# A four-stage block kernel: norm moves one cycle sooner, operands on another queue, stores kept back, weight lows on one engine

## The chip, the cores and the metric

The kernel runs on one core of a Trainium2 chip as one program. The metric is the device time of one execution in microseconds (us). Before the change three runs took 958.97 to 959.96 us, with a median of 959.61 us.

A core has five engines with an instruction queue each: TensorE (PE; its weight loads are listed as PEld), VectorE (DVE), ScalarE (ACT), GpSimd (POOL) and SyncE (SP). Each works through its own queue in order and waits at semaphores for the others. Transfers are issued here from SP's queue and from GpSimd's queue, and run on 16 DMA engines.

## The reference, cut to what matters

`x` is 2 x 1024 tokens of 512 numbers, float32.

```python
x = x + attn_a(layernorm(x))   # 4 heads, gated linear attention in chunks of 128 tokens
x = x + ffn(layernorm(x))      # 512 -> 1408 -> 512, integer weights with scales
x = x + attn_b(layernorm(x))   # one head of 512, softmax over 1024 keys, no mask
x = x + ffn(layernorm(x))      # the same ffn weights again

def attn_b(x):                 # per batch
    Q, K, V = x @ W_q, x @ W_k, x @ W_v
    return softmax(Q @ K.T / sqrt(512)) @ V @ W_o

def ffn(x):
    W = lambda wq, s: (wq - 128.0) * s[:, None]
    h = silu(x @ W(wq_gate, s_gate).T) * (x @ W(wq_up, s_up).T)
    return h @ W(wq_down, s_down).T
```

## The kernel before, in words

**Numbers in two parts.** A float32 operand `v` is split into `hi` (ScalarE's cast to the rounded type `fp32r`, line 70) and `lo = v - hi` (a subtraction, line 71, on VectorE unless the call names GpSimd). `mm3` multiplies with three matmuls: hi by hi, hi by lo, lo by hi (lines 84 to 86). `load_split` loads a tile and splits it.

**Order.** The kernel is written as one list of steps. A planner then gives each engine its queue: it takes the steps in the order of writing, simulates their times with a cost model, and lets a later step go ahead on an engine where an earlier one isn't ready in the simulation. The queues that come out are fixed; on the chip each engine keeps to its own. `behind(inss)` holds instructions of its block behind given ones of the same engine. `array(fn)` does this for TensorE, so that the matrix work of the second attention goes in the order written. Tiles come from pools; a tile with a tag waits for the release of an earlier one with the tag, and a pool that is opened after others are closed takes their memory, so that its first writes wait for the last readers there. `wp` has 12 slots of 8 KB a partition for large operands. `psum` has eight banks.

**Stage 1, attn_a.** First `M = W_q W_k^T` for the second attention is computed (`weight_product`, into four PSUM banks `pM`), and `spill` splits it (casts on ScalarE, lows on VectorE) and stores it to `m_d` with eight DMAs. Meanwhile the first norm tiles are made and turned (`ln_tile`, tiles `xn_a`, `pxT_a`, `xh_a`, `xl_a`), and `load_wqkv` splits Wk, Wq and Wv, the odd ones of four on GpSimd. `kv_part` and `q_head` are the projections (`pWk`, `pWv`, `pq`), `gate_proj` and `gates` the gates (`pab`, `ab`, `pz`). Sixteen chunks follow. The last steps compute `W_v W_o` (`V`), which `spill` stores to `vo_d`, and prepare the first FFN's operands.

**Stages 2 and 4, the FFN** (names end in `f` and `g`). Two rounds `pr` of 1024 tokens. Each runs over 11 blocks `j` of hidden units, with seven products instead of eight of half-size blocks (`products`, tiles `pX`, `pY`, `pZ`, `pV`, line 326); then eight tiles of the down product (`po`, lines 881 and 882). `stationary(j, ...)` provides the weights of block j in a slot `wc`: in the first round of stage 2 it loads integer codes (`cg`, `cu`), casts them, and GpSimd forms four sums and differences (lines 309 to 312), and SP stores the result to `wc_d[j]` (line 313, 896 KB); later it loads them back (line 315). `finish` makes the hidden tiles `ha`, `hb` (pool `ffnh`) and their splits `hs` (pool `ffn1`). `combine` makes the token operands from the transposed tokens `xT`.

**Norm groups.** For the second attention and the FFNs a norm is taken in groups of four tiles: `ln_steps` gives eight steps, four `ln_norm` (load `xin`, statistics `bn`, the power `rs` on GpSimd, `xn`, and a transpose by 32 x 32 blocks into `y`) and four `ln_move`, each of four DMAs of 64 KB that put the blocks in place in `xT`. `y` has one buffer, `xin` two.

**Stage 3, attn_b** (per batch b). `v_tile` and `q_proj`, then four cycles of two query tiles each: `scores_head` (products `ps`, whose sums end at `summed`), the matrix work `between`, `scores_tail` with the softmax (`mx`, `nm`, `pe`). `probs_T` turns a tile of probabilities: a transpose by blocks on VectorE (`py`), a store to `p_d` (`p<-py`, 512 KB) and four reads (`raw<-p`), all on SP. `probs_split` makes `pth` and `ptl` of it, and `out_b(b, i)` is the product with V (`pob`). The residual rows `xrb` come on GpSimd's queue. `do(norm, n)` takes the next n norm steps, `do(moving, n)` the next n of `combine`.

In batch 1 the norm group of stage 4 is taken along: group 0 before cycle 0, two norms of group 1 after cycle 0, and the other two with all four moves after cycle 1. In batch 0 the second group's four norms are all taken before cycle 1, and its moves after it.

Of the kernel before, what the change touches and what calls it, by code (L numbers as in the profile page):

```python
# [9 lines left out]
F32 = mybir.dt.float32  # L10
F32R = mybir.dt.float32r
I32 = mybir.dt.int32
AF = mybir.ActivationFunctionType
# [21 lines left out]
def hybrid_block_kernel(ctx: ExitStack, tc: tile.TileContext, a, out):  # L35
# [25 lines left out]
    def behind(inss):  # L61

        es = ExitStack()
        for ins in inss:
            es.enter_context(tc.issue_after(ins))
        return es
# [20 lines left out]
        ends[id(ps)] = end  # L87
        return end

    ends, normed_x, parts = {}, [], []  # L90

    def new_xT(name):
        return tuple(slot(f"{n}_{name}").rearrange("p (k c) -> p k c", k=KD) for n in ("xh", "xl"))
# [96 lines left out]
    def ln_move(nm, st, b):  # L190

        if b == 0:
            lnT[nm, st] = slot(f"xT_{nm}{st}").rearrange("p (k c) -> p k c", k=KD)
        y = lnY[nm, st]
        xf = lnT[nm, st].bitcast(F32).rearrange("p k (i b q) -> p (k i) b q", i=ST, b=4)
        for c in range(4):
            sync = nm in "af" or (nm, st) in (("b", 0), ("b", 1), ("g", 3)) or ((nm, st) == ("b", 2) and c % 2)
            (nc.sync if sync else nc.gpsimd).dma_start(  # L198
                out=xf[32 * b : 32 * (b + 1), :, c, :],
                in_=y[32 * c : 32 * (c + 1), b].rearrange("p k i q -> p (k i) q"),  # L200
            )
# [94 lines left out]
        codes(sp, "stg", c, a["wd"][j], f"cd{j}")  # L296
        nc.sync.dma_start(out=wd_d[j], in_=c)

    def stationary(j, name, fresh=None, loaded=None):


        w = slot(f"wc{name}_{j}").rearrange("p (n c) -> p n c", n=8)
        if fresh or loaded:
            a21, a11, s1, s2, s3, a12, s4, a22 = (w[:, n] for n in range(8))
            for n, (dst, nm) in enumerate(((w[:, 1:6:4], "cg"), (w[:, 0:8:7], "cu"))):
                room = (loaded[n], None) if loaded else fresh
                codes(*room, dst, a["wgu"][j][:, n * 512 : (n + 1) * 512], f"{nm}{name}_{j}")
            f = lambda x: x.bitcast(F32)
            nc.gpsimd.tensor_tensor(s1, f(a21), f(a22), ALU.add)
            nc.gpsimd.tensor_tensor(s2, f(s1), f(a11), ALU.subtract)  # L310
            nc.gpsimd.tensor_tensor(s3, f(a11), f(a21), ALU.subtract)
            nc.gpsimd.tensor_tensor(s4, f(a12), f(s2), ALU.subtract)
            nc.sync.dma_start(out=wc_d[j], in_=f(w[:, 1:8]))
        else:
            nc.sync.dma_start(out=w[:, 1:8].bitcast(F32), in_=wc_d[j])
        return w

    def products(ps, w, nm, pr, n, first):
# [17 lines left out]
    with ExitStack() as actx:  # L336
# [42 lines left out]
        def load_wqkv(nm, staged=None):  # L379
            two = [slot(f"{nm}{n}") for n in range(2)]  # L380
            done = []
            wqkv[nm] = [two[k // 2][:, k % 2 * 1024 : (k % 2 + 1) * 1024] for k in range(KD)]
            for k in range(KD):
                w, eng = wqkv[nm][k], nc.gpsimd if k % 2 else None
                if staged is None:
                    _, load = load_split(w, sp, a[nm][k * P : (k + 1) * P, :], f"{nm}{k}", eng)
                else:
                    done.extend(split(w[:, 0:512], w[:, 512:1024], staged[:, k], eng))
            return load if staged is None else done
# [90 lines left out]
        def q_head(st, h):  # L480
# [8 lines left out]
            for k in range(KD):  # L489
# [7 lines left out]
                    k == 0,  # L497
                    k == KD - 1,
                )
            nc.scalar.activation(qTa[st][:, h, :], ps, AF.Identity, bias=bq_s[:, h : h + 1])  # L500
            if h == 1:
                gates(st)
            if h == 2 and st > 0:
# [183 lines left out]
            wq_loaded = nc.sync.dma_start(out=staged[:, m], in_=a["Wq"][m * P : (m + 1) * P, :]).ins  # L687
        with behind((end,)):
            kv_part(0, "Wk")
        with behind(load_wqkv("Wq", staged)):  # L690
            spill(ap, ("kT", "kw", "sdec", "at"), pm, m_d, "M")
        for i in range(4):
            ends.clear()
            q_head(0, i)
            with behind((wq_loaded, *ends.values())):
                for t in ((), (4,), (5,), (6, 7))[i]:
                    ln_tile(t)
        load_wqkv("Wv")
        kv_part(0, "Wv")
        decays(0)  # L700
# [69 lines left out]
    def ffn(src, dst, nm, wcs, moving, ended, after):  # L770

        with ExitStack() as fctx:
            fh = fctx.enter_context(tc.tile_pool(name=f"ffnh{nm}", bufs=1))
            f1 = fctx.enter_context(tc.tile_pool(name=f"ffn1{nm}", bufs=2))
            fw = fctx.enter_context(tc.tile_pool(name=f"ffnw{nm}", bufs=KH))
            fp = fctx.enter_context(tc.tile_pool(name=f"ffn{nm}", bufs=4))
            wd = []
            for pr in range(2):  # L780
# [47 lines left out]
                for j in range(KH):  # L828
# [21 lines left out]
                    with behind(ended if pr == 0 and j < 3 else ()):  # L850
                        while moving:
                            moving.pop(0)()
                        first = nm == "f" and pr == 0
                        plan = (0, 1, 1, 1, 2, 2, 2, 1, 1, 1, 2) if first else (1, 1, 1, 1, 2, 2, 1, 1, 1, 1, 2)
                        for _ in range(plan[j] if early else 0):
                            early.pop(0)()

                    late_wd = nm == "f" and j < KH - 1
                    for n in range(len(wd), max(0, 2 * (j - 4)) if late_wd else KH if nm == "f" else j + 1):
# [50 lines left out]
    with ExitStack() as bctx:  # L910
# [230 lines left out]
        for b in range(NB):  # L1141
# [35 lines left out]
            for i in (0, 1):  # L1177
                probs_T(b, i)
            do(norm, 2)
            cycle(b, 1, lambda: q_proj(b, 1, (2, 3)))  # L1180
            for i in (2, 3):
                probs_T(b, i)
            do(norm, 4 if b == 0 else 6)
            array(out_b, b, 0)
            if b:
                moving = combine("g", 0)
# [25 lines left out]
            do(moving, 6)  # L1212
        array(out_b, 1, 5)
        array(out_b, 1, 6)
        wcs = [stationary(n, "g0") for n in range(2)]
        ended = (array(out_b, 1, 7),)

    out_t = [out[t * P : (t + 1) * P, :] for t in range(NT)]
# [63 lines left out]
```

## Time and profile before

| | |
|---|---|
| median of 3 runs | 959.61 us (958.97 to 959.96) |
| the profiled execution | 959.36 us, its span 957.6 us, granted clock 0.995 |
| PE busy | 937.2 us, 98% |
| DVE, ACT, POOL busy | 724.8 us (76%), 411.4 us (43%), 235.4 us (25%) |
| DMA | 162.18 MB, 169 GB/s over the span |

The profile comes from one execution. Times inside it count from the start of the span. An entry such as `pob<-vh,pth` names the output tile and what it reads; `[4.28 <-ACT pth L70]` says that the engine was idle 4.28 us before it and that ScalarE's line 70, which wrote `pth`, ended that. SPq and POOLq are the queues from which SP and GpSimd issue transfers. The granted clock is TensorE's, as a share of full speed. A matmul's record covers its pipeline, so one of 0.39 us may start 0.23 us after the last; what counts for TensorE is the distance from start to start.

### The profile page before, as it was taken

To read this page: it belongs to the slowest core of one execution; us is meant where nothing else is said; L and a number is where in the kernel's file an instruction comes from. 1 tells how busy PE (TensorE), PEld (TensorE's weight loads), DVE (VectorE), ACT (ScalarE), POOL (GpSimd) and SP (SyncE) were. 2 spreads that over 40 slices of the span, in tenths; PEclk is the share of its full clock that TensorE was granted. 3 is DMA by queue.
4 is the path that set the end of the run, shared out by engine and by line. 5 is a ranking of instruction groups with operands and counts; after the bars stand their busy time and mean duration, and the time that the engine had idled before them with its cause. 6 is when DMAs were issued, how large, how long until landed. Compare 5 with 4: busy or idle time off the path is not lost.

```text
span 957.6 us, 13198 instructions
## 1 busy us (share of the span) xinstructions
PE 937.2 (98%) x4402; PEld 776.1 (81%) x4402; DVE 724.8 (76%) x1457; ACT 411.4 (43%) x795; POOL 235.4 (25%) x334
## 2 busy tenths in 40 slices
PE   9999999999999999999999999999988999999998
PEld 7788888888788878888888788888866888888887
DVE  7757767779999699778948778479764967976655
ACT  6544434335665344354234444244332443534421
POOL 6323323444563012110120402041400261001100
PEclk9999999999999999999999999999989999999999
DMA  9426456576798557733745979247966772573112
GB/s 338 158 90 160 148 122 174 190 188 203 283 356 274 119 178 270 202 51 142 263 79 85 172 162 242 66 79 154 184 123 228 288 194 53 186 256 132 39 61 84
DMA packets 214838, 162.18 MB, mean 169 GB/s; under 512 B 150961, under 2 KB 166641, under 8 KB 214769
## 3 DMA queue, kind: packets, MB, share of 16 engines
q1 hardware_dynamic: 211184, 152.41, 54.8%
q0 software_dynamic: 3584, 8.92, 4.8%
q8 instruction: 35, 0.57, 0.3%
q14 instruction: 35, 0.28, 0.1%
HBM read 104.76 MB, written 41.84 MB: 153 GB/s over the span
## 4 chain that ended last, share of the span: by engine, by line
PE 84%; DVE 6%; DMA 5%; SPq 3%; ACT 1%; issue 1%; POOL 0%; ACTq 0%; DVEq 0%
PE pog L882 4%; PE pog L881 4%; PE pVg L326 4%; PE pZg L326 4%; PE pXg L326 4%; PE pVf L326 4%; PE pof L882 4%; PE pof L881 4%; PE pXf L326 4%; PE pZf L326 4%; PE pob L86 2%; PE pob L84 2%; PE pob L85 2%; PE pYg L326 2%; PE pYf L326 2%; PE psV L980 2%
## 5 line engine op out<-in xcount | busy, mean ns | idle before, releaser
L881 PE MATMUL pog<-wdg,hsg 128*128 128x512 f32 (+1 forms) x165 | 60.3, 375 | 0.0
L882 PE MATMUL pog<-wdg,hsg 128*128 128x512 f32 (+1 forms) x165 | 60.2, 375 | 0.0
L881 PE MATMUL pof<-wdf,hsf 128*128 128x512 f32 x154 | 59.5, 390 | 0.7 <-ACT hsf L70 0.7
L882 PE MATMUL pof<-wdf,hsf 128*128 128x512 f32 x154 | 59.2, 390 | 0.0
L84 PE MATMUL pob<-vh,pth 128*128 128x512 f32 x128 | 51.3, 401 | 5.2 <-ACT pth L70 5.2
L86 PE MATMUL pob<-vh,ptl 128*128 128x512 f32 x128 | 51.0, 398 | 0.0
L85 PE MATMUL pob<-vl,pth 128*128 128x512 f32 x128 | 50.9, 397 | 0.0
L326 PE MATMUL pXg<-B_g,wcg 128*128 128x512 f32 x176 | 47.1, 392 | 3.4 <-DMA wcg<-wc 3.4
L71 POOL TENSOR_TENSOR hsg<-sgg,hsg 128x128 fp32r<-128x128 f32 x40 | 19.6, 509 | 124.7 <-ACT hsg L70 124.7
L326 PE MATMUL pVf<-T_f,wcf 128*128 128x512 f32 x176 | 46.4, 390 | 1.0 <-ACT hbf L811 1.0
L326 PE MATMUL pVg<-T_g,wcg 128*128 128x512 f32 x176 | 46.4, 389 | 0.0
L326 PE MATMUL pXf<-B_f,wcf 128*128 128x512 f32 x176 | 45.9, 391 | 0.4 <-DMA wcf<-wc 0.4
L109 POOL TENSOR_TENSOR rs_b<-ve_b,mhalf 128x1 f32<-128x1 f32 x16 | 12.3, 775 | 121.0 <-DVE ve_b L107 121.0
L326 PEld LDWEIGHTS pXg<-B_g,wcg 128*128 128x128 f32 x176 | 33.0, 188 | 10.7 <-DMA wcg<-wc 3.8
L326 PEld LDWEIGHTS pVf<-T_f,wcf 128*128 128x128 f32 x176 | 32.9, 188 | 8.3 <-ACT hbf L811 1.4
L198 POOL DMA_DIRECT2D xT_g<-y_g x48 | 31.1, 655 | 34.0 <-DVE T_b L71 21.0
L326 PEld LDWEIGHTS pXf<-B_f,wcf 128*128 128x128 f32 x176 | 32.9, 188 | 7.6 <-DMA wcf<-wc 0.8
L326 PEld LDWEIGHTS pVg<-T_g,wcg 128*128 128x128 f32 x176 | 33.0, 188 | 6.9
L70 ACT CAST pth<-raw 128x512 fp32r<-128x512 f32 x30 | 17.1, 618 | 49.5 <-DMA raw<-p 49.4
L1086 POOL DMA_DIRECT2D xrb<-x x16 | 9.2, 573 | 109.4 <-DMA x<-xrb 62.4
L881 PEld LDWEIGHTS pog<-wdg,hsg 128*128 128x128 f32 x165 | 31.1, 188 | 5.7
L882 PEld LDWEIGHTS pog<-wdg,hsg 128*128 128x128 f32 x165 | 31.0, 188 | 5.6
(337 smaller groups left out, 2767.5 us busy)
## 6 DMA issues: line engine op xcount, KB each, us to landing
wcg<-wc SPq DMA_DIRECT2D x22, 896.0 KB, 6.1
wc<-wcf SPq DMA_DIRECT2D x11, 896.0 KB, 5.7
wcf<-wc SPq DMA_DIRECT2D x11, 896.0 KB, 6.0
p<-py SPq DMA_DIRECT2D x15, 512.0 KB, 3.8
raw<-p SPq DMA_DIRECT2D x60, 128.0 KB, 4.1
xin_a<-in_x SPq DMA_DIRECT2D x16, 256.0 KB, 4.7
xra<-in_x SPq DMA_DIRECT2D x16, 256.0 KB, 2.7
row<-cl SPq DMA_DIRECT2D x16, 256.0 KB, 3.9
```

Of the source, the lines that this page charges most:

```text
L70: c = nc.scalar.copy(hi, src)
L71: return c.ins, (eng or nc.vector).tensor_tensor(lo, src, hi.bitcast(F32), ALU.subtract).ins
L84: nc.tensor.matmul(ps, lhs_hi, rhs_hi, start=first, stop=False)
L85: nc.tensor.matmul(ps, lhs_hi, rhs_lo, start=False, stop=False)
L86: end = nc.tensor.matmul(ps, lhs_lo, rhs_hi, start=False, stop=last).ins
L109: nc.gpsimd.tensor_tensor(rs, ve, mhalf, ALU.pow)
L198: (nc.sync if sync else nc.gpsimd).dma_start(out=xf[32 * b : 32 * (b + 1), :, c, :], in_=y[32 * c : 32 * (c + 1), b].rearrange("p k i q -> ...
L326: nc.tensor.matmul(ps, w[:, m, k * P : (k + 1) * P], o[:, s, k, :], start=first and k == 0 and s == 0, stop=k == 1 and s == 1, skip_group_ ...
L881: nc.tensor.matmul(ps, hs[i][0][:, j], wd[j][:, ds], start=j == 0, stop=False)
L882: nc.tensor.matmul(ps, hs[i][1][:, j], wd[j][:, ds], start=False, stop=j == KH - 1)
L980: ends[nm] = nc.tensor.matmul(ps, o[:, i, k], w[:, j, k], start=first and k == 0 and i + j == 0, stop=k == 1 and i == 1, skip_group_check= ...
L1086: nc.gpsimd.dma_start(out=xr, in_=x2[t])
```

## The change

- `load_wqkv`: the odd lows of Wk and Wq go from GpSimd to VectorE; those of Wv stay.
- `spill` of M is taken after the second head of `q_head(0, ..)`, behind its copy on ScalarE and the last norm on VectorE, and no longer right after the Wq splits.
- `stationary`: the store of line 313 is put on a list, and the FFN's block loop takes the oldest off it as long as more than two are left, and all in the last block.
- The pools `ffn1` and `ffnh` are opened in the other order, in both FFNs.
- `ln_move`: of the first norm group of stage 4 (`("g", 0)`) half of the DMAs go to SP, as already for `("b", 2)`.
- In batch 1 the third and fourth norm of group 1 are taken in cycle 1 after `q_proj`, behind the sums of the scores; after cycle 1 only the four moves are left.
- The first two operands `wc` of stage 4 are loaded from GpSimd's queue.

```diff
--- before.py
+++ after.py
@@ -87,7 +87,7 @@
         ends[id(ps)] = end
         return end
 
-    ends, normed_x, parts = {}, [], []
+    ends, normed_x, parts, copied = {}, [], [], []
 
     def new_xT(name):
         return tuple(slot(f"{n}_{name}").rearrange("p (k c) -> p k c", k=KD) for n in ("xh", "xl"))
@@ -194,7 +194,8 @@
         y = lnY[nm, st]
         xf = lnT[nm, st].bitcast(F32).rearrange("p k (i b q) -> p (k i) b q", i=ST, b=4)
         for c in range(4):
-            sync = nm in "af" or (nm, st) in (("b", 0), ("b", 1), ("g", 3)) or ((nm, st) == ("b", 2) and c % 2)
+            half = (nm, st) in (("b", 2), ("g", 0))
+            sync = nm in "af" or (nm, st) in (("b", 0), ("b", 1), ("g", 3)) or (half and c % 2)
             (nc.sync if sync else nc.gpsimd).dma_start(
                 out=xf[32 * b : 32 * (b + 1), :, c, :],
                 in_=y[32 * c : 32 * (c + 1), b].rearrange("p k i q -> p (k i) q"),
@@ -296,7 +297,9 @@
         codes(sp, "stg", c, a["wd"][j], f"cd{j}")
         nc.sync.dma_start(out=wd_d[j], in_=c)
 
-    def stationary(j, name, fresh=None, loaded=None):
+    saves = []
+
+    def stationary(j, name, fresh=None, loaded=None, queue=None):
 
 
         w = slot(f"wc{name}_{j}").rearrange("p (n c) -> p n c", n=8)
@@ -310,9 +313,9 @@
             nc.gpsimd.tensor_tensor(s2, f(s1), f(a11), ALU.subtract)
             nc.gpsimd.tensor_tensor(s3, f(a11), f(a21), ALU.subtract)
             nc.gpsimd.tensor_tensor(s4, f(a12), f(s2), ALU.subtract)
-            nc.sync.dma_start(out=wc_d[j], in_=f(w[:, 1:8]))
+            saves.append(lambda: nc.sync.dma_start(out=wc_d[j], in_=f(w[:, 1:8])))
         else:
-            nc.sync.dma_start(out=w[:, 1:8].bitcast(F32), in_=wc_d[j])
+            (queue or nc.sync).dma_start(out=w[:, 1:8].bitcast(F32), in_=wc_d[j])
         return w
 
     def products(ps, w, nm, pr, n, first):
@@ -381,7 +384,7 @@
             done = []
             wqkv[nm] = [two[k // 2][:, k % 2 * 1024 : (k % 2 + 1) * 1024] for k in range(KD)]
             for k in range(KD):
-                w, eng = wqkv[nm][k], nc.gpsimd if k % 2 else None
+                w, eng = wqkv[nm][k], nc.gpsimd if k % 2 and nm == "Wv" else None
                 if staged is None:
                     _, load = load_split(w, sp, a[nm][k * P : (k + 1) * P, :], f"{nm}{k}", eng)
                 else:
@@ -497,7 +500,7 @@
                     k == 0,
                     k == KD - 1,
                 )
-            nc.scalar.activation(qTa[st][:, h, :], ps, AF.Identity, bias=bq_s[:, h : h + 1])
+            copied[:] = [nc.scalar.activation(qTa[st][:, h, :], ps, AF.Identity, bias=bq_s[:, h : h + 1]).ins]
             if h == 1:
                 gates(st)
             if h == 2 and st > 0:
@@ -687,14 +690,16 @@
             wq_loaded = nc.sync.dma_start(out=staged[:, m], in_=a["Wq"][m * P : (m + 1) * P, :]).ins
         with behind((end,)):
             kv_part(0, "Wk")
-        with behind(load_wqkv("Wq", staged)):
-            spill(ap, ("kT", "kw", "sdec", "at"), pm, m_d, "M")
+        load_wqkv("Wq", staged)
         for i in range(4):
             ends.clear()
             q_head(0, i)
             with behind((wq_loaded, *ends.values())):
                 for t in ((), (4,), (5,), (6, 7))[i]:
                     ln_tile(t)
+            if i == 1:
+                with behind((*normed_x, *copied)):
+                    spill(ap, ("kT", "kw", "sdec", "at"), pm, m_d, "M")
         load_wqkv("Wv")
         kv_part(0, "Wv")
         decays(0)
@@ -772,8 +777,8 @@
 
 
         with ExitStack() as fctx:
+            f1 = fctx.enter_context(tc.tile_pool(name=f"ffn1{nm}", bufs=2))
             fh = fctx.enter_context(tc.tile_pool(name=f"ffnh{nm}", bufs=1))
-            f1 = fctx.enter_context(tc.tile_pool(name=f"ffn1{nm}", bufs=2))
             fw = fctx.enter_context(tc.tile_pool(name=f"ffnw{nm}", bufs=KH))
             fp = fctx.enter_context(tc.tile_pool(name=f"ffn{nm}", bufs=4))
             wd = []
@@ -854,6 +859,8 @@
                         plan = (0, 1, 1, 1, 2, 2, 2, 1, 1, 1, 2) if first else (1, 1, 1, 1, 2, 2, 1, 1, 1, 1, 2)
                         for _ in range(plan[j] if early else 0):
                             early.pop(0)()
+                    for _ in range(len(saves) if j == KH - 1 else len(saves) - 2):
+                        saves.pop(0)()
 
                     late_wd = nm == "f" and j < KH - 1
                     for n in range(len(wd), max(0, 2 * (j - 4)) if late_wd else KH if nm == "f" else j + 1):
@@ -1177,10 +1184,17 @@
             for i in (0, 1):
                 probs_T(b, i)
             do(norm, 2)
-            cycle(b, 1, lambda: q_proj(b, 1, (2, 3)))
+
+            def between():
+                q_proj(b, 1, (2, 3))
+                if b:
+                    with behind(summed):
+                        do(norm, 2)
+
+            cycle(b, 1, between)
             for i in (2, 3):
                 probs_T(b, i)
-            do(norm, 4 if b == 0 else 6)
+            do(norm, 4)
             array(out_b, b, 0)
             if b:
                 moving = combine("g", 0)
@@ -1212,7 +1226,7 @@
             do(moving, 6)
         array(out_b, 1, 5)
         array(out_b, 1, 6)
-        wcs = [stationary(n, "g0") for n in range(2)]
+        wcs = [stationary(n, "g0", queue=nc.gpsimd) for n in range(2)]
         ended = (array(out_b, 1, 7),)
 
     out_t = [out[t * P : (t + 1) * P, :] for t in range(NT)]
```

## The prediction

> **What bounds the kernel now.** I read the page first, then TensorE's waits, then the windows table by stage, and followed each wait back along the chain and the queues' timelines.
>
> ```profile
> PE 84%; DVE 6%; DMA 5%; SPq 3%; ACT 1%; issue 1%; POOL 0%; ACTq 0%; DVEq 0%
> ```
>
> The chain that ended last is TensorE for 84%. In steady stretches a 128x512 matmul starts every 0.227 us; only places where TensorE waits can give anything. They are (waiter <- releaser: us, times, longest):
>
> ```profile
> PE pob L84 <- ACT pth L70: 5.2, 2, 4.3
> PE pXg L326 <- DMA wcg<-wc: 3.4, 1, 3.4
> PE pxT_a L119 <- DVE xn_a L111: 1.3, 2, 0.9
> PE warm L660 <- POOL ones L343: 1.3, 1, 1.3
> PE pVf L326 <- ACT hbf L811: 1.0, 1, 1.0
> PE pz L418 <- DVE ab L410: 0.8, 1, 0.8
> PE pS L624 <- ACT kT L598: 0.8, 1, 0.8
> PE pof L881 <- ACT hsf L70: 0.7, 1, 0.7
> PE pab L406 <- DVE xl_a L71: 0.6, 1, 0.6
> PE pYf L326 <- POOL wcf L310: 0.5, 1, 0.5
> ```
>
> Some 16 us in all, and the change goes at all but the fourth, seventh and eighth. TensorE's timeline dates them: pz 30.83, pxT_a 32.29, pVf 256.37, pYf 262.46, pob 700.99 and 721.90, pXg 726.03. In the windows table (length, PE busy, PEld, DVE, ACT, POOL, granted clock, DMA share, GB/s) two stretches stand out:
>
> ```profile
> 0.00:44.00 44.00, 39.90 (x187) 32.00 (x188) 35.43 (x77) 25.88 (x46) 21.95 (x29) 1.00 0.77 269
> ...
> 692.00:747.00 55.00, 46.15 (x186) 36.41 (x185) 31.13 (x50) 18.36 (x31) 2.16 (x4) 0.91 0.70 199
> ```
>
> TensorE idles 4.1 and 8.9 us there, in the second with the clock at 0.91. Between them 240 to 270 lacks 1.5, and 640 to 692 nothing, but there VectorE is busy for 45.57 of 52 us (88%), with a DMA share of 0.89.
>
> **Part 1, the start (Wk and Wq lows on VectorE, M spilled later).** VectorE's timeline has two Wk lows:
>
> ```profile
> 16.96 3.38 DVE L71 TENSOR_TENSOR Wk<-stg_Wk,Wk 128x512 fp32r<-128x512 f32 x2
> ```
>
> That is 1.69 us for a subtraction that takes 0.68 with GpSimd idle; GpSimd's two (3.00 us from 16.79) run beside them. From 16.96 to 23.87 VectorE needs 6.91 us for two Wk, two Wq and two xl. With all eight weight lows and no GpSimd beside them it is ten at 0.60 us from start to start, 6.0 us: 0.9 earlier. By starts over the pace, TensorE loses 0.52 in pWk and 0.79 before pab here; I take 0.9 of the 1.31. Then the four M lows (2.4 us) leave the stretch 25.07 to 28.7, so ab and xn_a come 2.4 us sooner: pz's and pxT_a's waits, 0.99 and 0.97 by starts, go: 1.96. Given back: M's four casts (2.06 us on ScalarE) and four lows land at about 30 to 34, ahead of the Wv lows, which GpSimd ends at 39.28, while pWv (40.23 now) wants them 2.9 sooner: 0 to 2.9, I take 1.0, since Wv's loads are long there. M's PSUM banks, four of eight, stay taken some 5 us longer: 0 to 2, taken as 0, because pWk's, pab's and pq's banks are copied out by then. Its eight stores move behind on SP, ahead of the x tiles (32.26), which VectorE holds back anyway. Sum 1.9; ends -1.0 and 3.9.
>
> **Part 2, the first FFN's start (stores kept back, pools swapped).** SP's timeline:
>
> ```profile
> 245.01 0.32 SPq L313 DMA_DIRECT2D wc<-wcf  x1
> 245.43 1.79 SPq L655 DMA_DIRECT2D x<-xra  x1
> 247.31 0.42 SPq L172 DMA_DIRECT2D vo<-V  x1
> ...
> 253.10 0.61 SPq L284 DMA_DIRECT2D cgf<-in_wgu  x1
> ```
>
> SP stood at this wc store from 240.2 to 245.0, for GpSimd's differences; behind it wait the last x store (data there at 242.7), eight vo stores and the code loads. Without it the queue starts about 2.3 us sooner, and a second wc store (0.58) leaves it too. ScalarE's first hb (255.63) waits 3.1 us for vo stores: its memory is that of the V tiles. With the hs pool in front, hb lies farther up and its wait goes, or is for the first stores. The two TensorE waits, by starts 1.25 and 0.79 with the slow matmul behind each, are 2.04; I take 1.9 (0 if planned otherwise, 2.04 at most). The kept stores go out one or two rounds later, each 896 KB; their operands stay in their slots for the next round anyway, so that costs nothing, or the rounds' slack.
>
> **Part 3, the moves of the second norm group.** GpSimd's timeline, then the chain:
>
> ```profile
> 676.12 8.41 POOL L198 DMA_DIRECT2D xT_g<-y_g  x13 [6.64 <-PE psV L980]
> ```
>
> ```profile
> 684.89 6.33 DMA p<-py
> ...
> 696.77 3.45 DMA raw<-p
> ```
>
> Tile 4's probabilities are written while GpSimd's 16 moves of 64 KB run (676.1 to 687.0): from p's issue to the cast pth it takes 684.89 to 700.32, 15.4 us, where tile 2 took 662.82 to 673.57, 10.75. TensorE was ready at 696.32: 4.45 lost, and the next 12 matmuls start every 0.427 us, 2.55 more: 7.0. With the moves gone that 7.0 goes. But the norm steps now run inside cycle 1, and their x tiles are loaded at 653.59 behind SP's raw reads, landing 3.0 us later; with bn, rs, xn and transpose y is done near 661 (an estimate), and the moves then run beside tile 2's p. At tile 4's 15.4 us its cast starts at 678.25; out_b(1,2) starts at 675.85 and must have it at 675.2: 3.1 lost. The nearest row in code is batch 0, where the moves (525.72 to 536.0) end before p (536.10): 12.4 us, and TensorE lost 0.4. The other end: 3.7 us of norm work (two of 0.60, 0.08, 0.06, 0.46, 0.63) ahead of the softmax on a full VectorE: 6.8, and 2.5 of slow clock, 9.3. I take 3.1, as the moves overlap p, and 1.1 for the clock, between the wait of 1.37 (256.37; one slow matmul) and that of 3.80 (726.03; 1.6). Net 7.0 - 4.2 = 2.8; ends -2.3 and 6.6. The Trainium skill's page "TensorE: Matmul & The Clock Gate" (Part 1) gives an idle window of about 3.4 us before the clock halves; by it the 3.1 costs no clock, and the net would be 3.9. Half of the first group's moves go to SP, idle from 606.5 to 642.5: eight at 0.65 fit, and would cost 5.2 if p stood behind them.
>
> **Part 4, the second FFN's first operands on GpSimd's queue.** They wait on SP behind tile 7's raw reads and an x store until 718.87 and take 7.12 us. TensorE loses 3.57 at 726.03 and 1.68 in slow matmuls after it: 5.25. GpSimd's queue has only the xrb loads (704.6 and 712.6) between 687.5 and 745. The two loads are 1.8 MB, and may slow tile 7's p and raw as the moves slowed tile 4's: 0 to 4.7 (15.4 - 10.75), I take 1.25, for the reads' tail alone. So 4.0; ends 0.5 and 6.4 (with the 1.19 at 721.90, if the softmax of tile 7 comes up sooner). If the loads are planned ahead of an xrb load, that one waits for a slot too; its reader is VectorE's residual add. The page "DMA: Bandwidth & Descriptors" (Issuing engines are not separate DMA queues) speaks against this part: all queues end in the same 16 engines, and another issuer saves only the time of issuing. Here that is 1.36 us for the three issues; by it this term is 1.4 and the time 951.6. I hold to the row, since what is saved is the place behind the raw reads.
>
> **Sum.** 1.9 + 1.9 + 2.8 + 4.0 = 10.6 off the profiled 959.36 (span 957.6 and 1.8 around it), which lies 0.25 under the median of 959.61: 949.0. All ends together: 18.9 off, 940.7, or 2.8 on, 962.4.
>
> **Rivals.** (B) The wait moves with the moves: out_b(1,2) loses 9.3 as at its far end. For it: 88% busy VectorE, 0.89 DMA share in 640 to 692. Against: batch 0. Net 5.5: 954.1. (C) Operands and tile 7 collide: part 4 gives 0.5, 952.5. For it: the 7.12 us landing; against: TensorE has FFN products to put in between. (D) The planner leaves the moves where they are, since y still waits for the x tiles: part 3 is 0, 951.8. (E) Slower: the norm steps, now planned in front of the softmax, make VectorE stand. If bn_g is put right behind the sums that end at 649.1 and x lands at 656.6, VectorE stands 7.5; ptl of tile 0 is behind it, so out_b(1,0) (655.13) loses 7.5 and 2.5 of clock, and out_b(1,2) loses 9.3. Part 3 is then 7.0 - 10.0 - 9.3 = -12.3, and with the other 7.8 it is 4.5 on: 964.1. It decides once out_b(1,0) loses over 5.5, a stand of 3 us with its clock. For it: queues are in order and the order is fixed by a simulated time. Against: the same pairs of loads and norms at 643.9 and 664.0 show no stand.
>
> **How the numbers follow.** Forecast 0.58, B 0.14, C 0.10, D 0.02, E 0.16. What a measurement tells from no change is 0.2%, 1.9 us. A to D are faster but for 0.04 of their tails: 0.80 faster, 0.04 same, 0.16 slower. The range goes from 940.5 to 961.5: all ends good below; above, all ends bad, short of E's full price.
>
> **What would show it.** Right: no M lows between 25 and 28 and pz not waiting; no wait for vo at L811; moves between 655 and 675 and no wait over 1 us at out_b's fifth tile; wcg landed before TensorE asks, clock 1.0 there. Wrong: pob at tile 2 waiting for pth over 4 us; bn_g waiting for xin_g; pth of tile 7 over 2 us late; waits at pWv for Wv's lows.

## The result and the profile after

The changed kernel takes 959.56 us (median of 12 runs, 957.02 to 960.85), the kernel before 960.25 us beside it (12 runs, 956.64 to 963.28). The ratio is 0.999 with a 95% interval of 0.9976 to 1.0004: no change that this measurement can tell, where 949.0 us was forecast. The profiled execution took 958.89 us, its span 957.2.

The page's chain is as before, with a point less of VectorE and a point more of ScalarE:

```profile
PE 84%; DVE 5%; DMA 5%; SPq 3%; ACT 2%; issue 1%; POOL 0%; ACTq 0%
```

TensorE's waits (waiter <- releaser: us in total, times, longest) have changed places:

```profile
PE pob L84 <- ACT pth L70: 12.0, 2, 7.8
PE pxT_a L119 <- DVE xn_a L111: 1.4, 2, 1.0
...
PE pVf L329 <- ACT hbf L816: 1.2, 1, 1.2
...
PE pYf L329 <- POOL wcf L313: 0.9, 1, 0.9
```

Gone are the 3.4 us for `wcg` and the 0.8 at `pz`; the two waits for `pth` have grown from 5.2 to 12.0, and those at `pVf` and `pYf` are still there. In the windows table (length, PE busy, PEld, DVE, ACT, POOL, granted clock, DMA share, GB/s) the start has won 1.45 us of matmul time, while 640 to 692, where TensorE was busy all the time before, now lacks 4.1 us:

```profile
0.00:44.00 44.00, 41.35 (x196) 32.87 (x197) 33.60 (x83) 26.23 (x49) 16.02 (x26) 1.00 0.76 269
...
640.00:692.00 52.00, 47.88 (x202) 38.35 (x201) 41.64 (x96) 22.16 (x54) 14.46 (x23) 0.97 0.87 158
692.00:747.00 55.00, 47.17 (x203) 38.09 (x202) 36.62 (x60) 19.05 (x32) 3.22 (x6) 0.94 0.83 223
```

I set each matmul of one trace beside the same matmul of the other and took the difference of their starts. It says where the time went (changed kernel minus before, times of the kernel before):

| place | difference after it | step |
|---|---|---|
| 45 us | -2.05 | the start's gain |
| 248 us | -1.80 | 0.25 lost in the chunks |
| 262 us, first FFN's start | -0.95 | 0.85 lost: `pVf` and `pYf` wait a little longer than before |
| 410 us, second round of FFN 1 | -1.98 | 1.03 gained from 344 us on, most of it at 364, where `wcf` is there |
| 545 us | -2.39 | 0.41 gained at `out_b(0,2)` |
| `out_b(1,2)` | +3.65 | 6.04 lost: a wait of 4.29, then slow matmuls |
| `out_b(1,4)` | -2.99 | 6.65 gained: no wait |
| `out_b(1,7)` and the FFN behind it | -0.40 | 2.6 lost: a wait of 7.99 in place of 1.08 and 3.57, slow matmuls in both |
| end | -0.45 | |

Stretches of the same code differ between two profiles by up to 1.3 us at single places (at 344 us, for instance, where `pof` waits for `hsf`, and between 358 and 410 us), and the kernel before's first 45 us by up to 2 (experiment 13 runs them 2.0 us later than this profile). So rows of about 1 us are not certain one by one. The three large ones come back, with some spread, in the traces that have the same code at the place: 5.2 to 6.6 us at `out_b(1,2)` (seven traces) and 4.7 to 7.0 at `out_b(1,4)` in the old order (three traces), each a wait with the slow matmuls behind it, and a wait alone of 5.7 to 8.0 at `out_b(1,7)` (seven traces).

At the first of the large losses SP's and GpSimd's timelines show the two sets of transfers side by side:

```profile
665.01 14.47 SPq L1072 DMA_DIRECT2D raw<-p  x8
```

```profile
665.18 5.16 POOL L199 DMA_DIRECT2D xT_g<-y_g  x8 [2.73 <-issue]
671.37 3.24 POOL L199 DMA_DIRECT2D xT_g<-y_g  x5 [1.03 <-DMA xT_g<-y_g]
```

SP needs 14.47 us to issue the eight raw reads of tiles 2 and 3; before it took 7.34:

```profile
666.15 7.34 SPq L1065 DMA_DIRECT2D raw<-p  x8
```

From tile 2's `p` to its first `pth` cast done it is now 16.4 us (661.27 to 677.70), before it was 11.4 (662.82 to 674.20). At the second loss it is tile 7's four raw reads and the two operands. The kernel before's reads come first, then the changed kernel's reads and operands:

```profile
714.58 3.64 SPq L1065 DMA_DIRECT2D raw<-p  x4
```

```profile
713.83 8.65 SPq L1072 DMA_DIRECT2D raw<-p  x4
```

```profile
711.13 1.07 POOL L318 DMA_DIRECT2D wcg<-wc  x2
```

One of the changed kernel's four issues took 6.13 us, and `p` to the first `pth` took 15.5 us (710.20 to 725.74); before it was 10.6.

### The profile page after: what moved, and what is told of

Its sections match the earlier page's. It is cut to its first block, busy times and chain, and to the rows that moved or that the text cites. A ratio compares the mean times of both kernels' runs of the same rounds, so it can differ in the third digit from the quotient of the medians.

```text
span 957.2 us, 13215 instructions
## 1 busy us (share of the span) xinstructions
PE 934.8 (98%) x4402; PEld 775.2 (81%) x4402; DVE 721.6 (75%) x1461; ACT 412.4 (43%) x795; POOL 224.2 (23%) x324
## 4 chain that ended last, share of the span: by engine, by line
PE 84%; DVE 5%; DMA 5%; SPq 3%; ACT 2%; issue 1%; POOL 0%; ACTq 0%
PE pog L889 4%; PE pog L888 4%; PE pVg L329 4%; PE pZg L329 4%; PE pXg L329 4%; PE pXf L329 4%; PE pZf L329 4%; PE pVf L329 4%; PE pof L889 3%; PE pof L888 3%; SPq L1072 3%; PE pYg L329 2%; PE pYf L329 2%; DMA raw<-p 2%; PE pob L84 2%; PE pob L85 2%
## 5 line engine op out<-in xcount | busy, mean ns | idle before, releaser
L84 PEld LDWEIGHTS pob<-vh,pth 128*128 128x128 f32 x128 | 24.8, 194 | 18.0 <-ACT pth L70 13.0
L71 DVE TENSOR_TENSOR ptl<-raw,pth 128x512 fp32r<-128x512 f32 x30 | 19.6, 688 | 26.0 <-ACT pth L70 25.9
```

The source lines that it names most:

```text
L71: return c.ins, (eng or nc.vector).tensor_tensor(lo, src, hi.bitcast(F32), ALU.subtract).ins
L84: nc.tensor.matmul(ps, lhs_hi, rhs_hi, start=first, stop=False)
```

## The experiments

The theory after the first comparison: each part frees its own wait, but the moves and the operands were put beside the two transfers (tiles 2 and 7) that TensorE waits for next, and what was gained went there. Rivals: the norm steps ahead of the softmax load VectorE; or tiles 2 and 7 were late anyway and the waits only became visible. Each diff is against the changed kernel, but for experiments 1, 13 and 14, which edit the kernel before. "Span" is that of the profiled execution; 957.2 us for the changed kernel, 957.6 for the kernel before. Each ratio is to the kernel before, from runs taken beside it.

**1. The start alone, on the kernel before.** Edit: the hunks of the change that concern `load_wqkv`, `copied` and the place of `spill`, and nothing else.

> The kernel before with the start alone changed (odd lows of Wk and Wq on VectorE, M split and stored after the second head of q). In the changed kernel the same matmuls ran 2.05 us sooner by 45 us and 1.80 us sooner at 248 us. If this part earns that by itself and nothing downstream gives it back: no wait of TensorE at pz, every matmul from 45 us on 1.8 to 2.1 us sooner, and 957.8 us (957.3 to 958.4). Rival: the gain is given back at the first wait that follows a transfer (the first FFN at 256 us), since transfers and not TensorE set that moment: then 959.0 to 960.0.

Measured: 956.34 us, ratio to the kernel before 0.998 (0.9965 to 0.9996), span 954.1. By matched matmuls it is 1.97 us ahead by 45 us and 1.83 at 248, as in the changed kernel. Then it loses 0.4 up to `pYf`, 0.4 at `pof`, 0.5 at `pXf` (a wait for `wcf`) and 0.3 more, and at 410 to 550 it is only 0.16 ahead. Behind 701 us it is 2.9 ahead, because tile 4's wait was 3.1 us in this execution and not 4.4. So the start earns its 2 us, and the rival is half right: waits for transfers in the first FFN can take it back. And tile 4's wait, with no edit near it, differs by 1.4 us between two executions.

**2. The second group's moves on SP, behind the raw reads.**

```diff
-sync = nm in "af" or (nm, st) in (("b", 0), ("b", 1), ("g", 3)) or (half and c % 2)
+sync = nm in "af" or (nm, st) in (("b", 0), ("b", 1), ("g", 1), ("g", 3)) or (half and c % 2)
```

> The changed kernel with the sixteen moves of stage 4's second norm group on SP, where they stand behind the raw reads of tiles 2 and 3, instead of on GpSimd's queue beside them. Theory of the collision: tile 2's probabilities came late because the moves ran beside them on the same 16 DMA engines; now from tile 2's p to its pth about 11 us instead of 15.8, the wait of 4.3 us at out_b(1,2) and the slow matmuls after it go (6.0 us), and tile 4's wait stays away: 953.5 us (952.5 to 955). Rival, load of VectorE: the norms ahead of the softmax make py late, so the wait at out_b(1,2) stays over 3 us: 957.5 to 960. Second rival: the moves on SP hold up tile 4's p instead, and the wait appears at out_b(1,4), 3 to 7 us: 956.5 to 960.5.

Measured: 958.52 us, 1.0005 (0.999 to 1.0019), span 957.1. The wait at `out_b(1,2)` is gone: 6.0 us gained there against the changed kernel, with the norm steps still ahead of the softmax. That is against the load of VectorE and for the collision. But at `out_b(1,4)` 6.67 us are lost, as the second rival said. SP's timeline shows why:

```profile
679.51 5.37 SPq L199 DMA_DIRECT2D xT_g<-y_g  x7
684.98 1.04 SPq L1098 DMA_DIRECT2D x<-xrb  x2
687.25 0.32 SPq L97 DMA_DIRECT2D xin_g<-x  x1
687.67 1.02 SPq L1063 DMA_DIRECT2D p<-py  x2
```

Tile 4's `py` was done at 683.28; its `p` stood behind the moves, an x store, and an `xin` load that goes out as the first of the two stores lands (687.24): 4.4 us.

**3. The operands ahead of the last `xrb` load.**

```diff
-            (queue or nc.sync).dma_start(out=w[:, 1:8].bitcast(F32), in_=wc_d[j])
+            got = (queue or nc.sync).dma_start(out=w[:, 1:8].bitcast(F32), in_=wc_d[j]).ins
+            if queue:
+                fetched.append(got)
...
-        ended = (array(out_b, 1, 7),)
+        with behind(fetched):
+            ended = (array(out_b, 1, 7),)
```

> The changed kernel with the two first operands of stage 4 ahead of the last xrb load on GpSimd's queue, so that they start at about 704.5 us instead of 711.1, before tile 7's probabilities are written. Theory of the collision: tile 7's p to pth goes from 14.9 us to 11 to 12, the wait of 8.2 us at out_b(1,7) shrinks to 4 or 5, and the time falls by 3 to 4.5: 955.5 us (954.5 to 957). Rival: tile 7's reads are slow by themselves and only TensorE's lack of other work shows: no change, 959 to 960.

Measured: 953.93 us, 0.9946 (0.9925 to 0.9967), span 950.5. GpSimd's and SP's timelines:

```profile
704.14 1.07 POOL L318 DMA_DIRECT2D wcg<-wc  x2
```

```profile
709.96 0.37 SPq L1065 DMA_DIRECT2D p<-py  x1
713.89 2.82 SPq L1074 DMA_DIRECT2D raw<-p  x4
```

Seven microseconds earlier on the same queue, and the four raw reads are issued in 2.82 us and not 8.65; `p` to `pth` takes 10.4 us, `out_b(1,7)` waits 2.9, and the matmuls behind it are 6.5 us sooner. The theory holds, and its price was set too low. What is changed is only the place of 1.8 MB on GpSimd's queue.

**4. The operands back on SP.**

```diff
-wcs = [stationary(n, "g0", queue=nc.gpsimd) for n in range(2)]
+wcs = [stationary(n, "g0") for n in range(2)]
```

> The changed kernel with the two operands' loads back on SP, as before. If moving them to GpSimd's queue lost 2.6 us at out_b(1,7), as the comparison of the two traces says: wait at out_b(1,7) of about 1 us, a wait for wcg of about 3.4 us at the first FFN products, 957.0 us (956.3 to 957.8). Rival: the loss there came with the moved norm group and not with the queue: out_b(1,7) still waits over 5 us, 959 to 961.

Measured: 957.42 us, 0.9986 (0.9972 to 1.0001), span 955.7. The wait for `wcg` is back (3.6 us), that at `out_b(1,7)` is 2.1. Against the changed kernel 1.4 us in all, of which 0.7 were there before tile 7 and 0.7 came at it: the same sign as the 2.6 of the comparison, less in size, and within what one execution differs from the next. Here 14 slow matmuls (2.8 us) followed the wait for `wcg`, in the kernel before 9 (1.7).

**5. The moves held until tile 2's raw has landed, and halved.**

```diff
-            half = (nm, st) in (("b", 2), ("g", 0))
+            half = (nm, st) in (("b", 2), ("g", 0), ("g", 1))
...
+            gate = ()
+            if b:
+                seen = mp.tile([P, 1], F32, tag="rs", name="seen")
+                raw = ptT[NK + 2][2]
+                gate = (nc.gpsimd.tensor_tensor(seen, raw[:, 0, 0:1], raw[:, 0, 0:1], ALU.add).ins,)
+            with behind(gate):
+                do(norm, 4)
-            do(norm, 4)
```

> The changed kernel with the sixteen moves of stage 4's second norm group held until tile 2's raw has landed (a 128x1 addition on GpSimd reads it, the moves stand behind that), and halved between GpSimd's queue and SP behind the raw reads. Theory: two limits at once. Tile 2 is late in the changed kernel because the moves run beside it, and tile 4 is late with all moves on SP because its p stands behind them (issued at 687.7 us with py ready at about 683.5). Held and halved the moves run from about 674 to 680: out_b(1,2) waits under 1 us (6.0 us less), tile 4's p goes out at about 684 to 685 and out_b(1,4) waits 1 to 3 us: 955 us (953.5 to 956.5). Rival: what one tile gains the next loses whatever the moves do, since tile 4's chain from scores to pth takes as long as TensorE's work beside it and TensorE now comes 6 us sooner: wait at out_b(1,4) of 5 to 7 us, 958 to 960.

Measured: 956.97 us, 0.9982 (0.9969 to 0.9994), span 954.4. GpSimd's eight moves run where they were to (GpSimd's timeline), and `out_b(1,2)` has no wait (5.9 us gained):

```profile
672.61 0.18 POOL L1201 TENSOR_TENSOR seen<-raw 128x1 f32<-128x1 f32 x1 [10.13 <-DVE mx L1025]
673.17 5.17 POOL L199 DMA_DIRECT2D xT_g<-y_g  x8 [0.38 <-issue]
```

At `out_b(1,4)` 4.1 us go again: a wait of 2.8 and the slow matmuls behind it. Nothing holds SP's half back: two of its eight moves went out at 669.04, between the raw reads of tiles 2 and 3, and the other six took 6.87 us to issue from 673.81. `p`, ready at 681.98, went out at 684.59. So holding GpSimd's half takes the wait at tile 2 away, and SP is the wrong place for the other half.

**6. The last two blocks of V in another pool.**

```diff
-            hi, lo = (pool.tile([P, 512], F32R, tag=tags[m % len(tags)], ...) for j in range(2))
+            room = pool2 if pool2 and m > 1 else pool
+            hi, lo = (room.tile([P, 512], F32R, tag=tags[m % len(tags)], ...) for j in range(2))
...
-spill(ap, ("sq", "kT", "kw", "sdec"), next(prep)[0], vo_d, "V")
+spill(ap, ("sq", "kT", "state", "sWv"), next(prep)[0], vo_d, "V", a3)
```

> The changed kernel with the last two of the four blocks of V that are stored to vo in tiles of another pool (a3), so that only the first two lie in the pool whose memory hb takes. In the changed kernel hb's first write waited for the last vo store (issued 250.27, landed 253.92) although hb's addresses no longer meet that block's. Theory: the wait is for every reader of the closed pool, not for the addresses; with the last two blocks elsewhere hb waits for stores issued by 247.3 only, and the wait of 1.2 us at pVf goes: 1.0 to 1.5 us sooner behind 255 us, some of it given back at pYf 4 us later. Rival: something else holds hb, and the wait stays. By the time alone 957.5 to 960 either way; the trace decides.

Measured: 960.6 us, 1.0021 (1.0008 to 1.0035), span 958.5. ScalarE's timeline, the changed kernel first:

```profile
254.08 0.69 ACT L816 ACTIVATE hbf<-pZf,cols 128x512 f32<-128x512 f32 x1 [3.36 <-DMA cgf<-in_wgu]
```

```profile
251.46 0.69 ACT L817 ACTIVATE hbf<-pZf,cols 128x512 f32<-128x512 f32 x1 [0.73 <-DMA vo<-V]
```

`hb`'s wait is gone, 2.6 us sooner. (In the changed kernel the listing names a code load as the releaser; the last wait with a vo store in it ended at 253.92, as the store of 250.27 landed.) In the changed kernel `hb` waited for the stores of all four V blocks (the last landed at 253.90); with two blocks in another pool it waits for those of the other two (the last landed at 251.28). So the wait goes with the blocks that lie in the closed pool, and opening the pools in the other order did not take it away. I had worked out that `hb` lies over the first V block only, so that it would be the pool and not the addresses that counts; no trace shows the addresses, so that much is argued. And the gain did not come: the code loads now wait in `hb`'s place. SP issued the first of them at 253.94, just behind the landing of the last vo store (253.87), and not at 250.69, and TensorE's waits have a new one:

```profile
PE pXf L330 <- ACT wcf L294: 2.2, 1, 2.2
```

Behind 262 us the kernel is 1.2 us later than the changed one. My expectation had looked at `hb` alone.

**7. The wc stores not kept back.**

```diff
-            saves.append(lambda: nc.sync.dma_start(out=wc_d[j], in_=f(w[:, 1:8])))
+            nc.sync.dma_start(out=wc_d[j], in_=f(w[:, 1:8]))
```

> The changed kernel with the wc stores issued at once, as before, and all else kept. With the start alone changed, its 2 us shrank to 0.2 by 410 us, at waits for hsf, wcf and hbf; in the changed kernel 2.4 us were left at 545 us. Theory: keeping the stores back earned this 1.5 to 2 us, behind 262 us and not at the FFN's start where the sum put it: without it matmuls at 410 to 540 us run 1 to 2 us later than in the changed kernel, and the first x, vo and code issues after 240 us come 1.5 to 2.3 us later. Rival: these are differences from one execution to the next, and nothing moves by over 0.5 us.

Measured: 959.01 us, 0.9997 (0.9985 to 1.001), span 958.4. Up to 344 us nothing moves by over 0.6 us. At 363 us TensorE waits 0.9 us for `wcf<-wc`, which it doesn't in the changed kernel, and the matmuls from there are 1.0 us later than in the changed kernel, where they had been 0.2 sooner. So in this trace keeping the stores back earns about 1.2 us, 100 us behind the place where the sum had put it; the time, 959.01 against 959.56, doesn't show it. The wait itself comes back: all five traces without kept stores (the kernel before and experiments 1, 7, 13 and 14) have it, with 0.4 to 0.9 us, and of the eleven with them one (experiment 12, 0.3 us). The size is less sure, since experiment 12 too loses 1.3 us over this stretch.

**8. The norm group in its old place.**

```diff
-                if b:
-                    with behind(summed):
-                        do(norm, 2)
...
-            do(norm, 4)
+            do(norm, 4 if b == 0 else 6)
```

> The changed kernel with the second norm group in its old place (third and fourth norm and the moves after cycle 1). Theory: the wait moves from tile 2 back to tile 4: out_b(1,2) no wait, out_b(1,4) waits 4 us with slow matmuls after it, 6.0 gained and 6.65 lost against the changed kernel: 960.2 us by that, 959 to 961. Rival: without norm steps ahead of the softmax VectorE runs freer and both are on time: 953 to 955.

Measured: 955.28 us, 0.9958 (0.9942 to 0.9974), span 953.0: by the span 4.2 us less than the changed kernel. The time lies beside the rival's range, but not for its reason, since `out_b(1,4)` still waits. `out_b(1,2)` doesn't wait (6.0 gained), and at `out_b(1,4)` only 1.9 us are lost, not 6.65. The moves start 9.6 us ahead of tile 4's `p` (672.6 and 682.2), in the kernel before 8.8 (676.1 and 684.9): the planner, given the other parts of the change, had put the last transpose into `y` ahead of tile 2's `ptl`, where before it stood behind. So part of the old wait at tile 4 may have come from VectorE's order; experiment 13 tries that alone.

**9. Experiments 8 and 3 together.** Edit: both diffs.

> The changed kernel with the second norm group in its old place and the two operands of stage 4 ahead of the last xrb load. The profiles of the two edits alone gave 4.2 and 6.7 us less than the changed kernel's span of 957.2 us. If they add up: span 946.3 us, and by the 2.4 us between the changed kernel's span and its median 948.7 us (947 to 950.5); out_b(1,2) without a wait, out_b(1,4) waiting about 1.9 us and out_b(1,7) 2 to 3. Rival: TensorE reaches tile 7 sooner than its softmax lets it, and part of the 6.7 comes back as a longer wait there: 950.5 to 953.

Measured: 949.95 us (948.35 to 950.67), 0.9901 (0.9887 to 0.9916), span 949.0. This beats both kernels. TensorE's waits and the windows:

```profile
PE pob L84 <- ACT pth L70: 4.9, 2, 2.6
```

```profile
640.00:692.00 52.00, 52.00 (x228) 42.47 (x227) 44.73 (x99) 21.16 (x50) 14.57 (x23) 1.00 0.89 179
692.00:747.00 55.00, 50.09 (x209) 40.17 (x209) 39.78 (x68) 23.32 (x41) 6.09 (x12) 0.94 0.84 259
```

The gains add up but for 2.7 us of span (949.0 against 946.3): tile 4's wait is 2.5 us with 11 slow matmuls here, and not 1.9 with three, and tile 7's has 7 slow matmuls behind it where experiment 3 had three. Its second operand landed at 708.61, 3.3 us after tile 7's `p` was issued (705.33), and that store took 5.5 us to land, in experiment 3 3.8.

**10. The same, with half of the second group's moves on SP.** Edit: `("g", 1)` added to `half`, as in experiment 5.

> As the run before, and the sixteen moves of the second norm group halved between SP and GpSimd's queue, so that they take 5.3 us from about 672.6 and not 10.4, and are done before tile 4's p at about 682. Theory of the collision: out_b(1,4) then waits under 0.5 us, 1.9 to 2.5 us less than the run before: span 944.2 us, 946.5 us by the median (945 to 948). Rival: SP's eight moves stand in front of the x store and the xin load that precede tile 4's p in its queue, so p goes out 2 us later and the wait stays: no difference to the run before.

Measured: 952.07 us, 0.9923 (0.9909 to 0.9936), span 951.1: slower than the run before. The rival's mechanism, with a larger price: SP needs 10.42 us for its eight moves, while GpSimd's eight take 5.20 (671.95 to 677.15).

```profile
672.94 10.42 SPq L199 DMA_DIRECT2D xT_g<-y_g  x8
683.41 0.62 SPq L97 DMA_DIRECT2D xin_g<-x  x1
...
684.60 1.35 SPq L1065 DMA_DIRECT2D p<-py  x2
```

`py` was done at 681.65; `out_b(1,4)` waits 3.5 us.

**11. The last two blocks of V in the pool `rows`.** Edit: as experiment 6, with the tag `xres` of `rp` for blocks 2 and 3.

> The changed kernel with the last two blocks of V in tiles of the pool rows, which is not closed before the first FFN, so that neither hb nor the code loads can wait for their stores. Theory: hb's wait at pVf (1.2 us and a slow matmul, 1.4 in all) goes, but the next block's wcf, which comes by code loads, ScalarE's casts and GpSimd's sums, isn't sooner; pYf then waits for it 2.0 to 2.5 us and not 0.9: matmuls behind 262 us within 0.4 us of the changed kernel. Rival: without hb's wait ScalarE casts the codes sooner and both waits go: 1.4 to 2.2 us sooner.

Measured in one execution: span 960.0, 2.8 us more (1.2 of it at the start), and neither expectation. The wait at `pVf` is gone, but the pool has three buffers for four tiles, the last vo store goes out at 258.57, and TensorE has several waits of 0.7 to 1.6 us between 251 and 260. Inconclusive on what `hb`'s wait alone is worth.

**12. One operand on GpSimd's queue, one on SP.**

```diff
-stationary(n, "g0", queue=nc.gpsimd)
+stationary(n, "g0", queue=nc.gpsimd if n == 0 else None)
```

> The changed kernel with only the first of the two operands on GpSimd's queue, the second on SP as before. If tile 7's delay comes from the bytes that run beside it: 0.9 MB less beside p and raw, p to pth 12 to 13.5 us and not 15.5, the wait at out_b(1,7) 4 to 6 us and not 8.0, a wait for the second operand of 1 to 3 us after it. Rival, the queue itself (transfers from GpSimd's queue get ahead of SP's whatever their size): p to pth 15 us, wait 7.5 to 8.5 us.

Measured in one execution: span 955.5. `p` to `pth` takes 12.3 us, `out_b(1,7)` waits 3.5 us, and the second operand isn't waited for. The four raw reads were issued in 5.66 us:

```profile
713.99 5.66 SPq L1072 DMA_DIRECT2D raw<-p  x4
```

With none beside the reads (experiment 3, where the second operand still ran for the first 1.6 us of `p`) `p` to `pth` was 10.4 us, with two 15.5: in one trace each, the delay grows with the bytes, 0.9 MB for each step. That is against a rank of the queue that holds whatever the size, and for shared engines. Whether transfers from GpSimd's queue also go first isn't shown.

**13. The one swap on VectorE, on the kernel before.** Tile 2's `ptl` behind the last transpose into `y`.

```diff
-        nc.vector.transpose(lnY[nm, st][:, :, :, i, :], ...)
+        turned_y[:] = [nc.vector.transpose(lnY[nm, st][:, :, :, i, :], ...).ins]
...
-                        probs_split(b, i, summed)
+                        probs_split(b, i, (*summed, *turned_y) if (b, i) == (1, 2) else summed)
```

> The kernel before with one swap on VectorE in cycle 2 of batch 1: tile 2's ptl behind the last transpose into y. The moves then don't wait for tile 2's raw and start about 2.5 to 3.5 us sooner against tile 4's p. Theory: out_b(1,4) waits about 1.9 us with few slow matmuls and not 4.4 with twelve, 2.5 to 4.5 us gained there: 955.5 us (954.5 to 957.5). Rival: the old wait at tile 4 was in the moves' bytes and not in VectorE's order; the wait stays over 4 us, 958.5 to 960.

Measured: 958.61 us, 0.9983 (0.9966 to 1.0), span 956.5. At `out_b(1,4)` 4.5 us are gained: a wait of 2.1 us with three slow matmuls, where the kernel before has 4.4 with twelve. The wait is the theory's, the time the rival's: 1.7 us of the gain go at tile 7, whose `p` is only 1.2 us sooner (710.06, before 711.22, with TensorE 2.3 us earlier), and at the wait for `wcg` behind it, and this execution's start was 2.0 us late. The swap's size isn't settled either. With the slow matmuls, tile 4 lost 7.0, 4.7 and 5.4 us in the three traces with VectorE's old order (the kernel before, experiments 1 and 14), and 2.5, 2.3 and 4.5 in the three with the new one and all moves on GpSimd's queue (experiments 13, 8 and 9).

**14. The operands alone, ahead of the last `xrb` load, on the kernel before.** Edit: GpSimd's queue as in the change, and the diff of experiment 3.

> The kernel before with only the two operands on GpSimd's queue, ahead of the last xrb load (issued at about 705 us). Theory: the wait for wcg (3.6 us) and its slow matmuls (1.7) go, tile 7's p to pth stays at 10.6 us and its wait at 1 to 2 us: 954.3 us (953.5 to 956). Rival: the operands run beside tile 7's p (711.2) for some microseconds, pth comes 2 to 4 us later, and half is lost: 956.5 to 958.

Measured: 956.8 us, 0.9968 (0.9953 to 0.9984), span 953.1. There is no wait for `wcg`; `p` to `pth` takes 11.8 us and not 10.6, `out_b(1,7)` waits 2.3 and not 1.1, and 3.8 us net are gained at this place. The time is in the rival's range and the place between the two.

## Why the prediction was wrong, step by step

**Part 1 (forecast 1.9, measured 1.8 to 2.05, with an uncertainty as large, as the start varies): right.** In VectorE's timeline all four Wk lows now take less time than two had taken:

```profile
17.44 2.49 DVE L71 TENSOR_TENSOR Wk<-stg_Wk,Wk 128x512 fp32r<-128x512 f32 x4
```

`pz` doesn't wait. `pxT_a` still does (1.4 us), so of the 1.96 for the two waits only `pz`'s 0.99 came; and the 1.0 given back at pWv, for which no wait is seen, didn't come either. Two terms wrong by about 1 us cancel, so that the number is right in part by luck. The ends of this part, -1.0 and 3.9, don't follow from its terms, which give about -2.0 and 3.3; the measured gain lies inside both.

**Part 2 (forecast 1.9, measured about 0.2): wrong.** The step that failed is "with the hs pool in front, hb lies farther up and its wait goes". The vo stores went out 1.5 us sooner, not 2.3 (the last at 250.27, before at 251.80), but TensorE came 1.8 us sooner too, so the wait stayed: 3.36 us on ScalarE, before 3.11. It goes with the V blocks in the closed pool, and not with the place of `hb` in that memory as I had taken it (experiment 6). At the place itself 0.85 us were lost. The kept stores, costed at "nothing", earned about 1.0 us in the next round, by the table and experiment 7, which the sum had not looked at.

**Part 3 (forecast 2.8, measured 0.6): two terms.** The 7.0 regained at tile 4 was right (6.65), for the execution that the sum was read from; two others of the same order lost 4.7 and 5.4 there. The 4.2 lost at `out_b(1,2)` was mis-sized: 6.04. I had made the wait 3.1 from 15.4 us of collision (16.05 by the ends of the casts used here, and 16.43 now) and from a `p` that goes out when it did. But TensorE came 2.4 us sooner by then and `p` only 1.55: 3.1 + 0.85 + 0.4 is the 4.3 that was measured. The slow clock took 1.75 and not 1.1. The estimate that `y` is done near 661 was 3.6 us early too: the moves began at 665.18 and ran beside tile 2's raw reads, its `p` having landed at 664.96. What I had not seen at all is that part of the 7.0 at tile 4 was to be had by one swap on VectorE, without moving anything: 4.5 us against this profile, 2.2 and 2.9 against experiments 1 and 14 (experiment 13).

**Part 4 (forecast 4.0 gained, measured 2.6 lost by the trace and 0.7 at this place by experiment 4): the largest error, 4.7 to 6.6 us.** The gain was there to be had: 3.8 us net on the kernel before, where the loads are done early (experiment 14). The step that failed was "I take 1.25, for the reads' tail alone". The end that I had worked out for it, 4.7, is what was measured: 15.5 us from `p` to `pth` against 10.6. To that come 2.0 us from the parts in front: TensorE reached tile 7 3.0 us sooner, its `p` went out only 1.0 us sooner. Together they are the 6.9 by which the wait at `out_b(1,7)` grew, against the 3.6 of `wcg` that were saved. Across the traces this wait goes with the place of the operands: 5.7 to 8.0 us with both beside the reads (seven traces), 3.5 with one, 1.8 to 2.9 with both ahead (experiments 3, 9, 10 and 14). The Trainium skill's page "DMA: Bandwidth & Descriptors" (Issuing engines are not separate DMA queues) says that transfers from all queues end in the same 16 engines and interleave. The runs agree: with two, one and no operand beside them the raw reads took 8.65, 5.66 and 2.82 us to issue (3.64 in the kernel before, also with none). I had used the rule for the time of issuing that is saved, and not for the interleaving; the 1.4 us of gain that I had worked out from it had the wrong sign as well.

**The rivals.** B and C both came true in kind: B with 6.04 lost at `out_b(1,2)` of the 9.3 in its price, C beyond its price, with 2.6 lost where it had 0.5 gained. Taken together they stood in the prediction at 949.0 + 5.1 + 3.5 = 957.6 us, but no chance was given to that: each was priced as if the other stayed away, at 0.14 and 0.10. They have one cause, transfers put beside those that TensorE waits for next, and so should have had one chance. E didn't come: VectorE stood for no more than 0.8 us at a time between 640 and 672, and experiments 2 and 5 take the wait at tile 2 away with the norm steps left where they are.

**What stays open.** What `hb`'s wait would be worth alone wasn't shown, since both other places for V cost more than they gave. Nor was it shown why experiments 8 and 9, with the same moves, differ by 0.6 us and eight slow matmuls at tile 4.

## What to carry to other kernels

A transfer that is moved to another queue still runs on the same engines: before it is costed at nothing, name the next transfer that TensorE waits for, and see whether the two now overlap; the same loads 7 us earlier on the same queue were worth 6.5 us here. Where TensorE comes sooner by a gain upstream, ask of each later wait whether what it waits for comes sooner too. Where two rivals have one cause, price them together and give them one chance.

## What was not expected of the hardware

- **Issues stall behind traffic.** On SP's queue the issues of tile 7's raw reads took 0.32 to 1.01 us each in experiment 3, with no operand beside them, and up to 6.13 us in the changed kernel, beside the operands' 1.8 MB. In experiment 10, at the same time, eight moves took 5.20 us to issue on GpSimd's queue and 10.42 on SP's.
- **A wait of about 2 us can slow TensorE's clock, at no fixed threshold.** Over all these traces a wait of up to 1.6 us behind 240 us was followed as a rule by one or two slow matmuls (0.11 to 0.26 us). One of 1.81 us was followed by 9 matmuls of 0.43 us and so by 1.7 us, one of 1.87 by three (0.4), one of 2.47 by 11 (1.9), those of 2.07, 2.26 and 2.88 by three (0.4), those of 2.37, 2.77, 2.81 and 3.08 by 7 to 9 (1.6 to 1.8), and those over 3.4 by 7 to 14 (1.6 to 2.9). The Trainium skill's page "TensorE: Matmul & The Clock Gate" (Part 1) has an idle window of about 3.4 us that runs freely; that the price varies from wait to wait fits a free-running window, that waits of 1.8 and 2.5 us already pay it in full doesn't fit its length. The prediction's estimate by that page, no clock cost for a wait of 3.1 us, isn't borne out: the wait of 3.08 in experiment 1 cost 1.6 us.
